# Ten units of a grouped convolution moved between the steps of the last attention stage

## The chip, the cores and the metric

The kernel runs on one core of a Trainium2 chip. The metric is the time on the device in microseconds. The profile is of one execution; its span is 3171.0 us, and that execution was measured at 3172.86 us.

## The reference

Two layers work on two images of 256 channels and 64 x 64 pixels, all in 32-bit floating point.

Layer 0 is a masked global attention with 8 heads of 32 channels over 4096 pixels:

```
q, k, v = Wq x, Wk x, Wv x                       (1x1 convolutions)
fuse    = softmax(q k^T / sqrt(32)) v            (per image and head)
x       = (Wf [x, fuse]) * m + x * (1 - m)       (m: mask resized to 64 x 64)
```

Layer 1 multiplies x by a channel gate (two small matrices and a sigmoid), runs an attention inside windows of 8 x 8 pixels (4 heads of 64 channels), adds it to x, shuffles the channels, and ends with two grouped 7 x 7 convolutions whose groups have 4 channels:

```
y   = relu(bn1(conv7x7(x, sa_w1)))               (256 -> 64 channels, 64 groups)
y   = bn2(conv7x7(y, sa_w2))                     (64 -> 256 channels, 64 groups)
out = x * sigmoid(y)
```

## The kernel before, in words

A first part, up to about 160 us, projects q, k and v and writes them to DRAM. It also prepares the convolution weights. The rest is one function, `pipeline`, of which the program holds two versions (arm a without, arm b with a subtracted row maximum). The data of this case take arm a, and its tiles carry an a at the end of their names.

**Attention.** `pipeline` walks over 512 slots: 2 images x 8 chunks of 512 pixels x 2 groups of four heads x 32 blocks of 128 keys. A slot multiplies keys with queries (`scores`, tile sa), takes the exponential on ACT (ea), multiplies with the values (`products`, ava) and adds the exponentials on DVE (suma). The order of the instructions is the order in which the Python code emits them; nothing reorders them later, and each engine goes through its own list in order.

**Stages.** When a chunk of an image is through all its keys, small actions with a delay in slots follow (`at`, `later`): the denominators (dna), their reciprocal, their spread over the channels (rda), and the multiplication. Then a generator, `stage`, carries the chunk through the rest of layer 0 and through layer 1 up to the convolutions: fusion (hya), channel gate (ca1a, ca2a), window attention (qka, vwa, sca, ewa, pta, oa), output projection (opa), and the sum xo, which is written to a DRAM tensor `x_s` (xs). It has twelve steps, one each time it yields. During attention one step is emitted every four slots, so the stage of a chunk is hidden under the attention of the next. The last chunk of the second image has no next one: its denominators and its stage run alone.

**Convolutions.** `convolve` then runs 16 units. A unit has 4 output groups of the shuffled channels for both images. Rows lie on partitions: 128 partitions hold four sub-channels of 30 image rows and a margin, and three overlapping row blocks cover an image, so both images are 2 x 3 x 64 = 384 columns. A unit does:

- `load_x`: its rows from `x_s` into one of four x buffers (xca), one load of 420 KB for each image, on SP's queue
- `load_w`: banded weights of 896 KB (wa), eight units ahead, on SP's queue
- `conv1`: 28 matmuls into one PSUM bank (c1a), then a relu on ACT into one of two y buffers (yca)
- `conv2`: 28 matmuls into four banks (c2a), then two tanh and one scaling on ACT into one of two z buffers (za)
- `gate`: one multiplication of z by x on DVE, then 24 output DMAs, 12 issued from SP and 12 from POOL

The first convolution of unit u + 1 is emitted ahead of the second of unit u. The x buffer of unit u is free after its gate, and the loads of unit u + 4 are issued on SP after the twelve outputs of unit u. The profile counts each of these 32-bit matmuls as two, so a convolution shows as 56 of them.

The buffers of the convolutions lie where the attention had its keys, values, queries and exponentials. They can be filled only when the attention is over. POOL zeroes the four x and two y buffers then.

Of the kernel before, what the change touches and what calls it, by code (L numbers as in the profile page):

```python
# [28 lines left out]
NPIECE = NMB // PB  # L29
AHEAD = 2  # L30
EB = 5
WB = 8
HEADS1, HD1 = 4, 64
WS = 8
NW = W // WS
# [19 lines left out]
def conv_seq_kernel(ctx: ExitStack, tc: tile.TileContext, a, out):  # L55
# [411 lines left out]


    def pipeline(arm, shifted, pools):
        fp, xpool, gp, wp, avp = pools  # L470

        att = ExitStack()
        kvp = att.enter_context(tc.tile_pool(name=f"kv{arm}", bufs=AHEAD + 1))
# [120 lines left out]
        def products(i):  # L594
# [16 lines left out]
            if stop:  # L611
                if g == 0:
                    fts[b, c] = fp.tile([P, KC, CH], F32, tag="f", name=f"f{arm}_{b}_{c}")
                f = fts[b, c]
                nc.scalar.copy(f[:, g, :], av)  # L615
                if g == 0:
                    return
                both = [totals.pop((b, c, gg)) for gg in range(KC)]
                inv = fp.tile([P, P], F32, tag="inv", name=f"inv{arm}_{i}")
                rd = fp.tile([P, KC, 4, P], F32, tag="rd", name=f"rd{arm}_{i}")  # L620


                def denominators():
                    s = psum2(f"dn{arm}_{i}")
                    for h in range(HEADS0):
                        for q in range(4):
                            r = slice(32 * q, 32 * q + 32)
                            nc.tensor.matmul(
                                s[r, 0, 0:P],
                                keysum[:, h].rearrange("p i h -> p (i h)"),  # L630
                                both[h // HG][:, h % HG, q * P : (q + 1) * P],
                                start=(h == 0),
                                stop=(h == HEADS0 - 1),
                            )
                    nc.scalar.copy(inv, s[:, 0, 0:P])


                def spread(hh):
                    t = psum2(f"rd{arm}_{i}_{hh}")
                    for gg in range(KC):  # L640
                        for q in range(2):
                            r = slice(64 * hh + 32 * q, 64 * hh + 32 * q + 32)
                            nc.tensor.matmul(
                                t[:, q, gg * P : gg * P + P],
                                spread_h[r, gg].rearrange("p j d -> p (j d)"),
                                inv[r, :],
                                start=True,
                                stop=True,
                            )
                    nc.scalar.copy(  # L650
                        rd[:, :, 2 * hh : 2 * hh + 2, :],
                        t[:, :, 0 : KC * P].rearrange("p q (g n) -> p g q n", g=KC),
                    )

                at(2, denominators)
                at(3, lambda: nc.vector.reciprocal(inv, inv))
                at(4, lambda: spread(0))
                at(5, lambda: spread(1))
                at(6, lambda: nc.vector.tensor_mul(f, f, rd.rearrange("p g q n -> p g (q n)")))
# [207 lines left out]

        def convolve():  # L870
            psum_layout(f"conv{arm}", 3, 1)
            pool = att.enter_context(tc.tile_pool(name=f"conv{arm}", bufs=1))
            nb = len(BLOCKS)


            xcs, ycs = [], []
            for u in range(4):
                t = pool.tile([P, B * nb, UG, WP], F32, name=f"xc{arm}{u}")
                nc.gpsimd.memset(t, 0.0)
                xcs.append(t)  # L880
            for u in range(2):
                t = pool.tile([P, B * nb, WP], F32, name=f"yc{arm}{u}")
                nc.gpsimd.memset(t, 0.0)
                ycs.append(t)
            xs, ws, ys = {}, {}, {}
            dst = out.rearrange("b (g i) r w -> b i r g w", i=4)
            n64 = B * nb * W

            def load_w(u):
                if u < NU:  # L890
                    t = pool.tile([P, 2 * 32 * UW], F32, tag="w", name=f"w{arm}{u}", bufs=WB)
                    nc.sync.dma_start(t, w_s[u])
                    ws[u] = t

            def load_x(u, b):
                if u < NU:
                    x = xs[u] = xcs[u % len(xcs)]
                    nc.sync.dma_start(
                        x[:, nb * b : nb * b + nb].rearrange("p n g w -> p n (g w)"),
                        x_s[b, :, :, UG * u : UG * u + UG, :].rearrange("n p g w -> p n (g w)"),  # L900
                    )

            def conv1(u):
                if u >= NU:
                    return
                x = xs[u]
                w = ws[u][:, 0 : 32 * UW].rearrange("p (m g d) -> p g d m", g=UG, d=KS)
                s = psum1(f"c1{arm}{u}")
                for d in range(KS):
                    for j in range(4):  # L910
                        nc.tensor.matmul(  # L911
                            s[32 * j : 32 * j + 32, 0:n64],
                            w[:, j, d, :],
                            x[:, :, j, d : d + W],
                            start=(d == 0),
                            stop=(d == KS - 1),
                        )
                y = ys[u] = ycs[u % 2]
                nc.scalar.activation(
                    y[:, :, PAD : PAD + W],  # L920
                    s[:, 0:n64].rearrange("p (n x) -> p n x", x=W),
                    AF.Relu,
                    bias=cbias1[:, u : u + 1],
                )

            def conv2(u):
                y = ys.pop(u)
                w = ws.pop(u)[:, 32 * UW :].rearrange("p (m d) -> p d m", d=KS)
                tiles = [psum2(f"c2{arm}{u}_{hh}") for hh in range(2)]
                for d in range(KS):  # L930
                    for j in range(4):
                        r = slice(32 * j, 32 * j + 32)
                        nc.tensor.matmul(  # L933
                            tiles[j // 2][:, j % 2, 0:n64],
                            w[r, d],
                            y[r, :, d : d + W],
                            start=(d == 0),
                            stop=(d == KS - 1),
                        )
                z = pool.tile([P, 4, n64], F32, tag="z", name=f"z{arm}{u}", bufs=2)  # L940
                for hh in range(2):
                    nc.scalar.activation(  # L942
                        z[:, 2 * hh : 2 * hh + 2, :], tiles[hh][:, :, 0:n64], AF.Tanh, scale=0.5
                    )
                nc.scalar.activation(z, z, AF.Copy, bias=0.25, scale=0.25)  # L945
                return z.rearrange("p j (n x) -> p j n x", x=W)

            def gate(u, z):
                x = xs.pop(u)
                nc.vector.tensor_mul(  # L950
                    z, z, x[:, :, :, PAD : PAD + W].rearrange("p n g x -> p g n x")
                )
                for b in range(B):
                    for n, (x0, r0, r1) in enumerate(BLOCKS):
                        for i in range(4):
                            p = 32 * i + 1 - x0
                            eng = nc.sync if i >= 2 else nc.gpsimd
                            eng.dma_start(  # L958
                                dst[b, i, r0:r1, UG * u : UG * u + UG, :],
                                z[p + r0 : p + r1, :, nb * b + n, :],  # L960
                            )


            for b in range(B - 1):
                for u in range(len(xcs)):
                    load_x(u, b)
            for u in range(WB):
                load_w(u)
            yield
            for u in range(len(xcs)):  # L970
                load_x(u, B - 1)
            conv1(0)
            for u in range(NU):
                conv1(u + 1)
                z = conv2(u)
                load_w(u + WB)
                gate(u, z)
                for b in range(B):
                    load_x(u + len(xcs), b)

        def run_later():
            for _ in range(len(later)):
# [18 lines left out]
            scores(i)()  # L1001
        for i, (b, c, g, m) in enumerate(slots):
            now[0] = i
            if m % PB == 0:
                load_piece(i // PB + AHEAD)
            if g == KC - 1 and m == 0:
# [11 lines left out]
                next(banded, None)  # L1018
            if i % 4 == 0:
                run_stages()  # L1020
        while later:
            now[0] += 1
            run_later()
        psum.close()
        att.close()
        conv = convolve()
        next(conv)
        while stages:
            run_stages()
        for _ in conv:  # L1030
            pass
        psum.close()
# [2 lines left out]
    def arm(name, shifted):  # L1035
        with (
# [2 lines left out]
            tc.tile_pool(name=f"g{name}", bufs=1) as gp,  # L1039
            tc.tile_pool(name=f"w{name}", bufs=1) as wp,  # L1040
            tc.tile_pool(name=f"av{name}", bufs=1, space=PSUM) as avp,
            tc.manual_schedule(),
        ):
            pipeline(name, shifted, (fp, xpool, gp, wp, avp))

    safe = nc.values_load(flag[0:1, 0:1], min_val=0, max_val=1)
    with tc.If(safe > 0) as cond:
# [68 lines left out]
```

## Time and profile before

Three runs took 3169.08, 3174.86 and 3179.28 us; the median is 3174.86.

| engine | busy us | share of the span |
|---|---|---|
| PE (matmul) | 3054.3 | 96% |
| PEld (weight load, overlaps PE) | 1031.8 | 33% |
| DVE | 2552.5 | 80% |
| ACT | 2369.6 | 75% |
| POOL | 350.1 | 11% |

| stretch, us from the start | what runs | PE busy us | granted PE clock |
|---|---|---|---|
| 2724 to 2908 | attention of the last chunk, stage of the one before | 181.7 of 184 | 1.00 |
| 2908 to 2976 | denominators and stage of the last chunk | 42.0 of 68 | 0.75 |
| 2976 to 2989 | writing xo, loading the first rows of the second image | 0.6 of 13 | 0.65 |
| 2989 to 3151 | convolutions of 16 units | 156.9 of 162 | 0.97 to 1.00 |
| 3151 to 3171 | last gate and the last outputs | 0.1 of 20 | 0.57 |

Times in the profile are microseconds from the start of the span unless marked ns. A line of the timeline gives start, duration, engine, line of the kernel, operation, output and inputs, number of instructions merged, and in brackets the idle time before it with what ended it. A line of stretches gives, for each stretch, its length and the busy time and instruction count of PE, PEld, DVE, ACT and POOL, then the granted PE clock, the mean busy share of the 16 DMA engines and the GB/s that they moved. A line of a group gives the count, the total busy time and the mean of one in ns, and the idle time before. SPq stands for the queue on which SP issues DMAs; its duration is that of issuing, not of the transfer. PE being busy doesn't mean that it runs at its peak, since matmuls are pipelined and a slow clock makes them longer.

### The profile page before, as it was taken

How to read it: one execution, taken by the hardware profiler on the slowest of the kernel's cores; microseconds unless marked ns; L12 is line 12 of the kernel's file. 1: busy time of each engine (PE TensorE's matmuls, PEld its weight loads, DVE VectorE, ACT ScalarE, POOL GpSimd, SP SyncE). 2: the span in 40 equal slices, each digit the busy share in tenths (PEclk: the TensorE clock that was granted, in tenths of full speed). 3: DMA queues.
4: the chain of work that ended last, by engine and by line, in shares of the span. 5: the costliest groups of instructions: out<-in, count | busy, mean ns of one | idle time of the engine just before them, and what ended most of it. 6: DMA issues, size and time to landing. Idle time of an engine off the chain costs nothing.

```text
span 3171.0 us, 58707 instructions
## 1 busy us (share of the span) xinstructions
PE 3054.3 (96%) x24330; PEld 1031.8 (33%) x24330; DVE 2552.5 (80%) x1372; ACT 2369.6 (75%) x3574; POOL 350.1 (11%) x595
## 2 busy tenths in 40 slices
PE   8989999999999999999999999999999999998697
PEld 4442332323223232322322323223232323222365
DVE  3239989899898989898989899898989898987111
ACT  2239878787878888888888787878888888886233
POOL 7112001011020000000000000000000000001066
PEclk9989999999999999999999999999999999999798
DMA  6856124334261313122222221211312132222374
GB/s 201 338 158 80 55 64 62 67 65 65 63 77 57 74 58 74 57 68 64 58 67 58 64 65 54 69 56 61 75 57 74 57 74 57 62 64 76 108 213 109
DMA packets 160341, 264.04 MB, mean 83 GB/s; under 512 B 43945, under 2 KB 62621, under 8 KB 160065
## 3 DMA queue, kind: packets, MB, share of 16 engines
q1 hardware_dynamic: 133664, 221.72, 23.5%
q0 software_dynamic: 22432, 35.91, 7.8%
q8 instruction: 193, 3.16, 0.4%
q10 hardware_dynamic: 3968, 2.57, 0.3%
q14 instruction: 84, 0.68, 0.1%
HBM read 197.89 MB, written 65.21 MB: 83 GB/s over the span
## 4 chain that ended last, share of the span: by engine, by line
PE 56%; DVE 26%; issue 7%; DMA 4%; ACT 4%; POOL 2%; SPq 1%; DVEq 0%; ACTq 0%; POOLq 0%
DVE suma L607 23%; PE sa L576 21%; PE ava L605 18%; PE qka L741 3%; PE hya L672 3%; ACT ea L586 3%; PE vwa L759 2%; PE opa L837 1%; PE q L219 1%; DMA out_dram<-za 1%; PE k L219 1%; POOL out_dram L958 1%; PE v L244 1%; DMA ks<-kst 1%; PE c2a L933 1%
## 5 line engine op out<-in xcount | busy, mean ns | idle before, releaser
L607 DVE TENSOR_TENSOR suma<-suma,ea 128x2048 f32<-128x2048 f32 x960 | 2199.0, 2291 | 99.4 <-ACT ea L586 12.3
L586 ACT ACTIVATE ea<-sa 128x512 f32<-128x512 f32 (+1 forms) x3072 | 2044.6, 748 | 182.8 <-DVE suma L607 116.6
L576 PE MATMUL sa<-qa,ka 32*128 32x512 f32 x8192 | 1250.1, 641 | 13.0 <-DMA va<-vs 7.8
L605 PE MATMUL ava<-ea,va 128*32 128x512 f32 x8192 | 1093.0, 605 | 4.4 <-ACT fa L615 4.4
L576 PEld LDWEIGHTS sa<-qa,ka 32*128 32x128 f32 x8192 | 370.1, 183 | 803.0 <-ACT ea L586 676.8
L605 PEld LDWEIGHTS ava<-ea,va 128*32 128x32 f32 x8192 | 161.6, 108 | 784.8 <-issue 753.8
L863 POOL DMA_DIRECT2D xs<-xo x94 | 65.8, 707 | 2486.1 <-DVE xo L848 2486.1
L950 DVE TENSOR_TENSOR za<-za,xca 128x1536 f32<-128x1536 f32 x16 | 28.1, 1759 | 149.3 <-ACT za L945 70.7
L741 PE MATMUL qka<-ua,qkv_w 128*128 128x512 f32 x256 | 121.1, 617 | 2.6 <-DVE ua L733 2.6
L958 POOL DMA_DIRECT2D out_dram<-za x192 | 107.9, 571 | 77.0 <-DVE za L950 62.4
L750 ACT ACTIVATE qka<-qka,qkv_b 128x512 f32<-128x512 f32 x64 | 40.5, 683 | 89.2 <-PE qka L741 89.2
L911 PE MATMUL c1a<-xca,wa 128*32 128x384 f32 x896 | 79.5, 504 | 17.5 <-DMA xca<-xs 14.8
L680 ACT ACTIVATE ta<-hya,bf 128x512 f32<-128x512 f32 x32 | 20.2, 683 | 101.1 <-PE hya L672 101.1
L788 DVE TENSOR_REDUCE mxwa<-ewa 128x16 f32<-128x1024 f32 x16 | 19.5, 1220 | 93.0 <-ACT ewa L786 93.0
L607 DVE TENSOR_TENSOR suma<-ea,ea 128x2048 f32<-128x2048 f32 x32 | 73.1, 2285 | 14.9 <-DMA mca<-masks 14.9
L684 DVE TENSOR_TENSOR ta<-ta,mca 128x512 f32<-128x512 f32 x32 | 22.0, 688 | 74.6 <-ACT ta L680 74.6
L231 ACT ACTIVATE qsq<-q,bq 128x512 f32<-128x512 f32 x32 | 22.0, 687 | 79.0 <-DVE qst L230 77.5
L933 PE MATMUL c2a<-yca,wa 32*128 32x384 f32 x896 | 79.9, 498 | 0.3 <-ACT za L942 0.3
L428 POOL DMA_DIRECT2D ws<-r2s x112 | 69.3, 622 | 61.7 <-DMA ws<-r2s 29.6
L933 PEld LDWEIGHTS c2a<-yca,wa 32*128 32x128 f32 x896 | 71.1, 303 | 10.7 <-issue 9.0
L942 ACT ACTIVATE za<-c2a 128x768 f32<-128x768 f32 x32 | 24.2, 809 | 66.2 <-DMA out_dram<-za 34.2
L741 PEld LDWEIGHTS qka<-ua,qkv_w 128*128 128x128 f32 x256 | 47.2, 194 | 76.7 <-issue 49.1
(137 smaller groups left out, 1615.0 us busy)
## 6 DMA issues: line engine op xcount, KB each, us to landing
ka<-ks SPq DMA_DIRECT2D x256, 256.0 KB
va<-vs SPq DMA_DIRECT2D x256, 256.0 KB
ws<-zero POOLq DMA_DIRECT2D x16, 896.0 KB, 22.8
wa<-ws SPq DMA_DIRECT2D x16, 896.0 KB
xca<-xs SPq DMA_DIRECT2D x32, 420.0 KB
xs<-xo POOLq DMA_DIRECT2D x78, 140.0 KB, 6.4
x<-in_x_dram SPq DMA_DIRECT2D x16, 512.0 KB
ks<-kst SPq DMA_DIRECT2D x32, 256.0 KB
```

Source lines behind the costliest of these rows:

```text
L219: nc.tensor.matmul(s[:, g, :], w[:, kc, g * P : (g + 1) * P], rhs, start=(kc == 0), stop=(kc == KC - 1),)
L428: nc.gpsimd.dma_start(band2[:, at0 : at0 + step * (n - 1) + 1 : step, :], spread(r2_s[k : k + 1, :, i], n),)
L576: nc.tensor.matmul(heads[j], k[r, cols], q[r, g, :], start=True, stop=not shifted)
L586: nc.scalar.activation(e[:, h, :], tile, AF.Exp, scale=SCALE0)
L605: nc.tensor.matmul(av[r, :], v[:, m % PB, r], e[:, j, :], start=start, stop=stop)
L607: nc.vector.tensor_add(total, first[0] if m == 1 else total, e)
L672: nc.tensor.matmul(s[:, oc, :], wf[:, kc, oc * P : (oc + 1) * P], xw[kc] if kc < KC else f[:, kc - KC, :], start=(kc == 0), stop=(kc == 2 ...
L741: nc.tensor.matmul(s[:, j, :], wqkv[:, kc, o : o + P], u[:, kc, :], start=(kc == 0), stop=(kc == KC - 1),)
L863: eng.dma_start(x_s[b, n, p + r0 : p + r1].rearrange("r g w -> g r w"), xo[64 * h : 64 * h + 64, oc, r0 - WS * c : r1 - WS * c, :],)
L911: nc.tensor.matmul(s[32 * j : 32 * j + 32, 0:n64], w[:, j, d, :], x[:, :, j, d : d + W], start=(d == 0), stop=(d == KS - 1),)
L933: nc.tensor.matmul(tiles[j // 2][:, j % 2, 0:n64], w[r, d], y[r, :, d : d + W], start=(d == 0), stop=(d == KS - 1),)
L958: eng.dma_start(dst[b, i, r0:r1, UG * u : UG * u + UG, :], z[p + r0 : p + r1, :, nb * b + n, :],)
```

## The change

The convolutions become 26 items in place of 16 units. Items 0 to 9 are units 0 to 9 of the first image alone, items 10 to 19 the same units of the second image alone, and items 20 to 25 are units 10 to 15 of both images as before. An item of one image has 192 columns, 12 output DMAs (6 from SP, 6 from POOL) and one x load.

- The generator `convolve` is started in the last chunk's attention: it zeroes the two y buffers and loads the rows of units 0 to 2 of the first image and the weights of unit 0. Its buffers for these come from a pool of their own that exists all the time. There are three x buffers in place of four, and they are not zeroed.
- The first convolution of item 0 is emitted right after the last matmuls of the attention, ahead of the denominators. After the denominators the attention's buffers are given up, the weights of units 1 to 9 are loaded into nine buffers (eight before), and the first convolution of item 1 is emitted.
- Then one piece of the convolutions (a `conv1`, or a `conv2`; the gate with its outputs and the next x load goes ahead of the `conv1`) is emitted after each remaining action and each step of the stage: `conv2` of item 0 ahead of the spread of the denominators, and so on, up to `conv1` of item 9 after the output projection.
- After the stage's last step, `conv2` of item 8 and its gate follow, then the first x loads of the second image, `conv1` of item 10, `conv2` of item 9 and the rest of the items.
- The weights of units 1 to 9 stay until the second image has used them. The weights of units 10 to 15 are each loaded after the gate of unit 1 to 6 of the second image, ahead of the next x load.

```diff
-WB = 8
+WB = 9
+EARLY = 10
...
+        items = [(u, (b,)) for b in range(B) for u in range(EARLY)]
+        items += [(u, tuple(range(B))) for u in range(EARLY, NU)]
+        staged = []
...
-            for u in range(4):
-                t = pool.tile([P, B * nb, UG, WP], F32, name=f"xc{arm}{u}")
-                nc.gpsimd.memset(t, 0.0)
-                xcs.append(t)
+            for k in range(3):
+                xcs.append(cpool.tile([P, B * nb, UG, WP], F32, name=f"xc{arm}{k}"))
...
+            def load_rows(k):
+
+                while len(xs) < min(k + 1, len(items)) and (
+                    staged or B - 1 not in items[len(xs)][1]
+                ):
+                    load_x(len(xs))
...
-            for u in range(NU):
-                conv1(u + 1)
-                z = conv2(u)
-                load_w(u + WB)
-                gate(u, z)
-                for b in range(B):
-                    load_x(u + len(xcs), b)
+            load_rows(len(xcs) - 1)
+            load_w(0)
+            yield
+            conv1(0)
+            pool = yield
+            for u in range(1, 1 + WB):
+                load_w(u)
+            for k, (u, images) in enumerate(items):
+                while len(xs) <= k + 1 < len(items):
+                    yield
+                    load_rows(k + 1)
+                conv1(k + 1)
+                yield
+                z = conv2(k)
+                yield
+                gate(k, z)
+                if B - 1 in images and u:
+                    load_w(u + WB)
+                load_rows(k + len(xcs))
...
+            if (b, c, g, m) == (B - 1, NCHUNK - 1, 0, 0):
+                conv = convolve()
+                next(conv)
...
-        while later:
+        now[0] += 1
+        run_later()
+        next(conv)
+        while totals:
             now[0] += 1
             run_later()
         psum.close()
         att.close()
-        conv = convolve()
-        next(conv)
-        while stages:
+        psum_layout(f"conv{arm}", 3, 1)
+        conv.send(att.enter_context(tc.tile_pool(name=f"late{arm}", bufs=1)))
+        while later or stages:
+            now[0] += 1
+            run_later()
             run_stages()
+            if later or stages:
+                next(conv)
+        staged.append(True)
         for _ in conv:
             pass
```

## The prediction

> **What bounds the kernel now.** I read the page first. Its second part has PE in the nines in nearly every slice, then a dip near the end. Next come busy times by stretch around that dip:
>
> ```profile
> core 0: us, PE busy (x) PEld busy (x) DVE busy (x) ACT busy (x) POOL busy (x), PEclk, DMA share, GB/s
> 2724.00:2908.00 184.00, 181.74 (x1483) 54.23 (x1478) 167.42 (x85) 153.12 (x234) 8.29 (x12) 1.00 0.23 59
> 2908.00:2976.00 68.00, 41.96 (x347) 23.18 (x338) 20.37 (x16) 12.92 (x20) 6.60 (x6) 0.75 0.34 134
> 2976.00:2989.00 13.00, 0.59 (x4) 0.24 (x8) 1.29 (x2) 1.15 (x2) 1.39 (x2) 0.65 0.46 115
> 2989.00:3054.00 65.00, 64.25 (x728) 42.51 (x720) 8.80 (x5) 19.11 (x22) 31.24 (x56) 0.97 0.54 163
> 3054.00:3102.00 48.00, 43.91 (x512) 30.05 (x509) 8.79 (x5) 17.43 (x20) 31.23 (x57) 1.00 0.70 207
> 3151.00:3171.00 20.00, 0.12 (x2) 0.00 (x0) 1.76 (x1) 2.55 (x3) 12.88 (x24) 0.57 0.28 57
> ```
>
> Attention fills PE until 2908. Then comes an 80 us hole (the last stage, a serial chain at a half-warm clock), then 162 us of convolutions, then 20 us in which only outputs leave. The change works on all three. The reader should see that the hole is not empty: PE is busy 42 of 68 us, partly because the clock is 0.75.
>
> What paces the convolutions is in the timeline of one turn of an x buffer, in the middle stretch:
>
> ```profile
> 3047.76 1.76 DVE L950 TENSOR_TENSOR za<-za,xca 128x1536 f32<-128x1536 f32 x1 [7.81 <-DMA out_dram<-za]
> 3050.50 9.33 SPq L958 DMA_DIRECT2D out_dram<-za  x12
> 3059.88 0.92 SPq L898 DMA_DIRECT2D xca<-xs  x2
> 3064.72 4.81 PE L911 MATMUL c1a<-xca,wa 128*32 128x384 f32 x56 [0.80 <-DMA xca<-xs]
> ```
>
> The gate of unit 4 frees x buffer 0, SP issues twelve outputs, only then the two loads of unit 8, and PE waits for them: 15.2 us from gate end to conv1. This loop goes round four buffers, so it barely binds. Units start 9.65 us apart when PE sets the pace and 10.5 to 11.5 us apart where the loop does. Last, the parts of a unit, from the groups by form and the lines of the weight tile:
>
> ```profile
> L911 PEld LDWEIGHTS c1a<-xca,wa x896: 132/137/177, 2988.4 to 3139.6; 128*32 128x32 f32 x180
> L933 PEld LDWEIGHTS c2a<-yca,wa x896: 298/302/325, 3001.1 to 3150.3; 32*128 32x128 f32 x180
> L933 PE MATMUL c2a<-yca,wa 32*128 32x384 f32 x896 | 79.9, 498 | 0.3 <-ACT za L942 0.3
> L933 PEld LDWEIGHTS c2a<-yca,wa 32*128 32x128 f32 x896 | 71.1, 303 | 10.7 <-issue 9.0 <-ACT za L942 0.8
> ```
>
> For c2, weight loads run 71.1 of the 79.9 us of its matmuls: they are just hidden under 384 columns.
>
> **What the Trainium skill says.** *TensorE: Matmul & The Clock Gate*, "LDWEIGHTS", makes a load's time a matter of its columns. The trace agrees (about 190 ns for 128 columns, 110 for 32, both contiguous) and adds that c2's weights, read 28 bytes apart, take 302. The same page, "What's actually happening", halves the clock after an idle window. Here the first conv1, after 12.6 us of idling, takes 7.22 us instead of 4.83. *DMA: Bandwidth & Descriptors*, "Issuing engines are not separate DMA queues", has all issuers share the 16 engines; the DMA share of 0.70 in the middle stretch fits. *Perfetto Trace Analysis*, "Identifying Performance Opportunities", reads a bubble that repeats on an engine as too few buffers; the trace shows such bubbles already with four x buffers (0.80, 1.43 and 1.87 us at 3064, 3085 and 3097). After the change there are three.
>
> **The change part by part** (all against the profiled span of 3171.0; the runs read 3169 to 3179, median 3174.9).
>
> *Sizes.* Ten units are split by image: 192 columns instead of 384. A conv1 of 384 is 14 rounds of 0.328 us plus 0.23. With half the stream, 14 x 0.164 + 0.25 = 2.55 us; its loads (0.16 us per round) just fit. For c2 the stream would give 2.6 us, the loads at their full 302 ns 4.5. Loads overlap somewhat (contiguous 128-column loads of 190 ns follow each other every 0.12 to 0.13 us), so I scale 302 ns to 0.25 us per round: 3.85 us, ends 2.6 and 4.5. So a split unit costs 6.4 us per image, 12.8 for both, where it cost 9.65: about 31 us more PE work over ten units. After c2 there are tanh 1.0, copy 0.8, gate 0.9 and hand-overs (half of 1.51, 1.49 and 1.76, a little over), together 2.75 us. Six outputs on SP take 2.75 us (twelve took 5.04 to 5.82 where nothing held them), POOL's six 3.4.
>
> *Before the hole.* Three x loads, w0 and the two y memsets move into attention: 2.2 MB is 5.2 us at the 420 GB/s reached at 2930, ahead of k and v loads issued two pieces (some 19 us) early. I take nothing; bound 5. The four x memsets (5.8 us on POOL) go; denominators and stage chain hide them.
>
> *The hole.* PE's order is fixed: conv1 of unit 0 right after attention, while DVE still sums (free); denominators end at 2919.5; then conv1 of unit 1, in front of everything in the chain. Its weights wait for the attention buffers, released at 2919.5 as the memset of x was before. Issue, about 1.8 us until bytes moved then, 2.2 us for 917 KB: conv1(1) at about 2924.0, cold. From there PE runs one conv piece between every two stage steps: eight conv1 (5.0 cold + 7 x 2.55 = 22.9), eight conv2 (8 x 3.85 = 30.8), the stage's matmuls warm (0.5, 0.5, 6.9, 1.05, 1.05, 3.63, 3.63, 3.65, 1.15, 2.1, 1.15, 3.7 = 29.0). Waits add 3.6: 2.7 for x of unit 3, whose issue sits on SP behind nine weight loads, 20 us of transfers; 0.9 for unit 8. Sum 86.2, so the output projection ends at 3010.2, where it ended at 2975.8: **34 us later**. Some of the stage's ACT and DVE work queues behind tanh and gates (exp waits for tanh of unit 5), but PE is the longer queue. Ends: 20 later with c2 at stream speed, 40 with full loads.
>
> *End of the stage.* Before, 12.6 us passed from there to the first conv1 of the second image. After, that load is issued behind the six outputs of unit 8, which wait for conv1(9) 2.55, conv2(8) 3.85, ACT and DVE 2.75, SP 2.75; then load and landing 4.0: 15.9 us. It starts at **3026.1** against 2988.4.
>
> *Second image and both.* With three buffers, x of item k+3 is issued after the gate of item k, which follows conv1(k+1) and conv2(k). So two starts later, conv1(k+3) waits for 2.55 + 3.85 + 2.75 + 2.75 + 0.46 + 3.8 = 16.2 us. Where a weight load is issued in front of it (units 1 to 6, 917 KB), 0.42 for issue and 1.5 of its 2.2 us make 18.1. That is 8 to 9 us per split unit, where PE needs 6.4. Starts after 3026.1: 8.9, 18.6, 25.1, 36.7, 43.2, 54.8, 61.3, 72.9, 79.4, then the both-image units at 90.2, 98.9, 109.7. For those the loop is 4.8 + 4.9 + 4.75 + 5.6 + 0.92 + 3.8, 24.8 us per two: 123.7, 134.5, 148.5; the last conv2 ends at 163.5. Before it was 162.2. Image 0's work is out of this phase, and nothing is gained, because the loop has fewer buffers and shorter turns to hide the same latency.
>
> *Tail.* From the last conv2, 4.75 + 0.3 + 6.7 (POOL) + 7.1 to the end as before = 18.9; before 20.4, as POOL was one unit behind.
>
> Sum: 3026.1 + 163.5 + 18.9 = 3208.5, or **37.5 us more**. A measured time lies 1.9 above its span in the profiled run: 3210.
>
> **The rivals.**
> - *PE sets the pace of the second image* (faster). Loads land within PE's own time: the projection ends at its early bound, 20 us later (2995.8), the second image starts 13.7 after it, at 3009.5; cold start 2.4, conv2(9) 2.6, ten units of 5.0, six of 9.75, total 113.5; tail 18.9: 3142, time 3144. It decides if everything after conv2 (gate, outputs, landing, 9.8 us) takes no more than one PE unit, 5.0 to 6.4. For it: the added work lies in a hole that was 40% idle. Against it: no landing in the trace is under 3.4 us from issue (2984.93 to 2988.41 on an empty queue).
> - *Halves are cheap, the loop is at its floor* (about the same). c2 2.7, ACT and DVE 2.6, SP 2.6, landing 3.6: 7.0 us per unit, 8.0 with weights. The stage is 22 us late, the phase takes 145 instead of 162, the tail saves 1.5: span 3174, time 3176.
> - *The loop is slower still.* PE idles 3 to 5 us per pair; if the clock drops (the transposes took 3.68 after 7.6 us of idling, 2.08 warm) and full weight loads hold (4.5), a split unit takes 10 us: 3235.
> - That the change doesn't do what it says is excluded: the order of the instructions shows the conv pieces between the steps.
>
> **How the numbers follow.** Forecast case (3190 to 3222) 0.61, cheap halves 0.15, slower loop 0.13, PE pace 0.11. Faster by over 0.3% (under 3165; about what this kernel's measurement can tell from no change): the PE pace and a sliver of cheap halves, 0.13. Within 0.3%: most of cheap halves, 0.13. Slower: 0.74. The range 3168 to 3236 leaves out the faster cases and the far end of the slow one.
>
> **What would show it.** The output projection ending near 3010; conv1 of 192 columns at 2.5 and conv2 at 3.9 us; c1 waiting on xca in most of the second image's units, at a spacing near 8 to 9 us; PE busy about 75% there. A spacing of 5 to 6.5 us, or a stage delayed by 20 us or less, makes it wrong on the fast side.

## The result and the profile after

The changed kernel takes 3228.61 us (median of four runs, 3227.55 to 3229.07). The four runs of the kernel before that it is set against have a median of 3177.07 us (3169.08 to 3183.15). The ratio is 1.0163, with a 95% interval from 1.0139 to 1.0187: the change makes the kernel **1.6% slower**. The forecast was 3210, with a range of 3168 to 3236.

Below, each kernel is compared through its own ratio to the runs of before that were made beside it, because the median of before differed by up to 8 us between sets of runs (3177, 3173, 3169). Places in time are from one profiled execution of each; the span of the changed kernel is 3225.8 us.

The stretches of the changed kernel, with the same columns as those of before (length, busy time of PE, PEld, DVE, ACT and POOL, granted PE clock, DMA share, GB/s):

```profile
core 0: us, PE busy (x) PEld busy (x) DVE busy (x) ACT busy (x) POOL busy (x), PEclk, DMA share, GB/s
2724.00:2908.00 184.00, 181.74 (x1484) 53.73 (x1480) 167.53 (x84) 154.59 (x236) 8.19 (x13) 1.00 0.27 70
2908.00:2976.00 68.00, 51.43 (x666) 36.34 (x663) 24.10 (x18) 17.92 (x33) 11.15 (x20) 0.85 0.46 160
2976.00:3010.00 34.00, 32.77 (x603) 27.11 (x605) 8.28 (x9) 13.25 (x21) 13.50 (x24) 1.00 0.30 70
3040.00:3100.00 60.00, 45.58 (x747) 38.78 (x744) 6.72 (x7) 14.98 (x28) 20.22 (x36) 0.86 0.45 132
```

The attention's last chunk (first row) is what it was: PE is busy for 181.74 of 184 us in both kernels. The stage that follows is fuller, but also longer. And where before had a convolution phase at a clock of 0.97 to 1.00 with PE busy 64 of 65 us, PE now idles for a quarter of the time (45.6 of 60 us) and is granted 0.86.

Three of the costliest PE groups of the page, kept apart by shape (count, busy us, mean ns, then the idle time ahead of them by what ended it), say which operation pays:

```profile
L951 PE MATMUL c2a<-yca,wa 32*128 32x192 f32 x1120 | 72.3, 401 | 0.0
L927 PE MATMUL c1a<-xca,wa 128*32 128x192 f32 x1120 | 64.9, 390 | 41.6 <-DMA xca<-xs 30.7 <-issue 6.2 <-DMA wa<-ws 4.7
L927 PE MATMUL c1a<-xca,wa 128*32 128x384 f32 x336 | 33.2, 551 | 16.2 <-DMA xca<-xs 16.2
```

The first convolution waits for rows of x, 30.7 us ahead of the split units and 16.2 us ahead of those for both images. The second one waits for nothing. The same from PE's view, the waits between 2905 and 3226 us (total us, times, longest):

```profile
PE c1a L927 <- DMA xca<-xs: 47.0, 11, 9.3
PE c1a L927 <- issue: 6.2, 1, 6.2
PE c1a L927 <- DMA wa<-ws: 4.7, 1, 4.7
```

One such wait in the timeline, with what stands ahead of it on the other engines:

```profile
3073.54 3.57 PE L951 MATMUL c2a<-yca,wa 32*128 32x192 f32 x56
3077.03 2.53 PE L927 MATMUL c1a<-xca,wa 128*32 128x192 f32 x56
3079.50 3.58 PE L951 MATMUL c2a<-yca,wa 32*128 32x192 f32 x56
3088.61 4.71 PE L927 MATMUL c1a<-xca,wa 128*32 128x192 f32 x56 [5.53 <-DMA xca<-xs]
...
3078.92 0.96 DVE L973 TENSOR_TENSOR za<-za,xca 128x768 f32<-128x768 f32 x1 [13.16 <-ACT za L967]
3079.91 2.46 SPq L979 DMA_DIRECT2D out_dram<-za  x6
3082.47 0.36 SPq L899 DMA_DIRECT2D wa<-ws  x1
3082.87 0.43 SPq L906 DMA_DIRECT2D xca<-xs  x1
```

The gate frees the x buffer at 3079.88. SP issues six outputs, a weight load and then the x load, which is landed 5.3 us after its issue ended. PE could have used the rows at 3083.08, when conv2 was through; it stood still for 5.53 us. The conv1 that follows takes 4.71 us, where the one that finds PE running takes 2.53. The same columns of stretches, for the wait and for that conv1:

```profile
3083.10:3088.60 5.50, 0.00 (x0) 0.03 (x1) 0.96 (x1) 1.71 (x3) 2.91 (x6) 0.88 0.89 282
3088.61:3093.25 4.64, 4.64 (x57) 2.90 (x57) 0.00 (x0) 0.00 (x0) 0.90 (x2) 0.50 0.87 257
```

While PE waits the clock is still granted at 0.88; in the conv1 behind the wait it is 0.50. Below, *cold* means an operation that runs at such a lowered clock after idling, and *warm* one at the full clock of 1.00.

The whole difference of the two spans, 54.8 us, in sections:

| section | before | forecast | after | after less before |
|---|---|---|---|---|
| start to the end of the attention (copy of fa starts) | 2908.7 | 2908.7 | 2914.3 | +5.6 |
| to the end of the output projection | 67.1 | 101.5 | 103.1 | +36.0 |
| to the first conv1 of the second image | 12.6 | 15.9 | 15.3 | +2.7 |
| to the end of the last conv2 | 162.7 | 163.5 | 173.6 | +10.9 |
| to the end | 19.9 | 18.9 | 19.5 | -0.4 |

The first row can't be told from scatter, so it isn't shown to be an effect of the change. The copy of fa starts at 2903.8, 2906.4, 2908.2, 2909.2 and 2908.1 in the profiles of experiments 1, 2, 3, 4 and 6, all of which have the changed kernel's attention (experiment 2 with six smaller x loads in it); before's 2908.7 lies among them. Experiment 5, which has the attention of before, starts it at 2903.2, 5.5 us away from before itself.

### The profile page after: what moved, and what is told of

It is laid out like the page before. It is cut to its first block, busy times and chain, and to the rows that moved or that the text cites. A ratio compares the mean times of both kernels' runs of the same rounds, so it can differ in the third digit from the quotient of the medians.

```text
span 3225.8 us, 61120 instructions
## 1 busy us (share of the span) xinstructions
PE 3085.0 (96%) x25450; PEld 1077.1 (33%) x25450; DVE 2554.2 (79%) x1382; ACT 2376.3 (74%) x3614; POOL 344.5 (11%) x591
## 4 chain that ended last, share of the span: by engine, by line
PE 55%; DVE 27%; ACT 4%; issue 4%; DMA 2%; SPq 1%; POOL 0%; DVEq 0%; ACTq 0%
DVE suma L609 24%; PE sa L578 20%; PE ava L607 18%; PE qka L745 4%; PE hya L676 4%; ACT ea L588 3%; PE c1a L927 2%; PE c2a L951 2%; PE vwa L763 2%; PE opa L841 2%; DMA xca<-xs 1%; DMA ka<-ks 1%; SPq L979 1%; PE rda L647 1%; PE ca2a L719 0%
## 5 line engine op out<-in xcount | busy, mean ns | idle before, releaser
L609 DVE TENSOR_TENSOR suma<-suma,ea 128x2048 f32<-128x2048 f32 x960 | 2199.0, 2291 | 103.7 <-ACT ea L588 16.7
L973 DVE TENSOR_TENSOR za<-za,xca 128x768 f32<-128x768 f32 (+1 forms) x26 | 29.7, 1144 | 215.3 <-ACT za L967 184.9
L927 PE MATMUL c1a<-xca,wa 128*32 128x192 f32 (+1 forms) x1456 | 98.1, 427 | 57.8 <-DMA xca<-xs 47.0
L745 PE MATMUL qka<-ua,qkv_w 128*128 128x512 f32 x256 | 118.4, 605 | 0.0
L951 PE MATMUL c2a<-yca,wa 32*128 32x192 f32 (+1 forms) x1456 | 102.6, 424 | 0.3 <-ACT za L961 0.3
L951 PEld LDWEIGHTS c2a<-yca,wa 32*128 32x128 f32 x1456 | 94.5, 317 | 11.4 <-issue 10.2
L927 PEld LDWEIGHTS c1a<-xca,wa 128*32 128x32 f32 x1456 | 65.0, 148 | 86.7 <-issue 72.4
L935 ACT ACTIVATE yca<-c1a,cbias 128x192 f32<-128x192 f32 (+1 forms) x26 | 11.9, 459 | 109.5 <-PE c1a L927 109.5
L684 ACT ACTIVATE ta<-hya,bf 128x512 f32<-128x512 f32 x32 | 20.2, 683 | 97.8 <-PE hya L676 97.8
L961 ACT ACTIVATE za<-c2a 128x384 f32<-128x384 f32 (+1 forms) x52 | 26.6, 562 | 80.1 <-PE c2a L951 49.0
L792 DVE TENSOR_REDUCE mxwa<-ewa 128x16 f32<-128x1024 f32 x16 | 19.5, 1220 | 82.8 <-ACT ewa L790 82.8
```

The source lines that it names most:

```text
L609: nc.vector.tensor_add(total, first[0] if m == 1 else total, e)
L745: nc.tensor.matmul(s[:, j, :], wqkv[:, kc, o : o + P], u[:, kc, :], start=(kc == 0), stop=(kc == KC - 1),)
L927: nc.tensor.matmul(s[32 * j : 32 * j + 32, 0 : n * W], w[:, j, d, :], xs[k][:, 0:n, j, d : d + W], start=(d == 0), stop=(d == KS - 1),)
L951: nc.tensor.matmul(tiles[j // 2][:, j % 2, 0 : n * W], w[r, d], y[r, 0:n, d : d + W], start=(d == 0), stop=(d == KS - 1),)
```

## The experiments

**The theory.** Two costs of about one size. First, the convolution pieces are put between the steps of a serial chain and lengthen it by nearly all their PE time, and what they save later is their own PE time, so the move by itself gains little. Second, three x buffers can't hide the turn from gate to landed rows, so the second phase, with ten units' worth of one image gone, is not shorter. **The rivals:** that splitting units makes PE work dear (strided weight loads under half a stream), and that the pieces between the steps are themselves what is lost.

### 1. A fourth x buffer

```diff
             pool = yield
+            xcs.append(pool.tile([P, B * nb, UG, WP], F32, name=f"xc{arm}3"))
             for u in range(1, 1 + WB):
```

> The changed kernel with a fourth x buffer, which comes from the pool that opens after the attention. Theory (the turn of an x buffer paces the convolutions): the turn of about 20 us, measured over two starts in the changed kernel, is spread over three, 6.7 us, or PE's own 6.1 if the clock stays up. The ten items of the second image take 61 to 68 us in place of 96, the six of both about 62 in place of 77; the output projection ends at most 5 us earlier (x of item 3 no longer waits). Time 3175 to 3190. Rival (SP's issuing, the DMA engines or PE itself set the pace): the spacing of the second image's items stays above 9 us and the time within 6 us of 3229.

Measured: 3175.09 us, ratio 1.0015 (1.0005 to 1.0025). As the theory had it, except that x of unit 3 is still late: its conv1 in the hole waits 5.30 us (6.16 in the changed kernel), as its load still stands behind the nine weight loads on SP. PE's wait for x between 2905 and 3170 us:

```profile
PE c1a L927 <- DMA xca<-xs: 12.8, 4, 9.1
```

The two groups of conv1, by shape:

```profile
L927 PE MATMUL c1a<-xca,wa 128*32 128x192 f32 x1120 | 58.1, 359 | 21.8 <-DMA xca<-xs 11.2 <-issue 5.3 <-DMA wa<-ws 4.7
L927 PE MATMUL c1a<-xca,wa 128*32 128x384 f32 x336 | 28.9, 492 | 1.6 <-DMA xca<-xs 1.6
```

And the stretch from 3034 to 3150 us, in the columns of the stretches above:

```profile
3034.00:3150.00 116.00, 111.40 (x1654) 90.01 (x1652) 18.40 (x15) 39.14 (x60) 63.07 (x114) 1.00 0.58 163
```

The wait for x falls from 47.0 to 12.8 us, and the groups lose most of theirs. In the last line's stretch PE was busy for 89.5 us in the changed kernel at a clock of 0.86; with one buffer more it is 111.4, at a full clock. The ten items of the second image take 66.8 us (96.1 in the changed kernel), and the phase up to the last conv2 129.2 (173.6). So this one buffer is worth nearly the whole loss. But the projection still ends 102.4 us after the attention. Against before, the hole costs 35.3 us more and the phase behind it 33.5 less: the move, freed of its missing buffer, gains nothing.

### 2. The same three buffers, cut in halves

An item of one image fills only half of a buffer that was laid out for two. Here an item of one image gets half a buffer, so six loads fit where three did; items of both images get whole ones.

```diff
-                x = xs[k] = xcs[k % len(xcs)]
+                h = part(k)
+                if len(h) == 2:
+                    x = xs[k] = xcs[h[0] // 2]
+                else:
+                    x = xs[k] = xcs[h[0] // 2][:, nb * (h[0] % 2) : nb * (h[0] % 2) + nb]
...
-                load_rows(k + len(xcs))
+                load_rows(ahead(k))
```

> The changed kernel with each of the three x buffers cut in two for items of one image, so that six such items find room; items of both images still have three. No memory is added. Theory: single items go at PE's pace, 6.1 us, so the second image's ten take about 62 us in place of 96; items of both images keep their 26 us per two. x of item 3 is there early, so the output projection ends about 6 us earlier. Time 3180 to 3195. Rival (landings are slow because the DMA engines are shared, whatever the number of buffers): still over 8 us per item, time above 3215.

Measured: 3176.38 us, ratio 1.0015 (1.0006 to 1.0025), a little better than expected. The groups of conv1 by shape:

```profile
L941 PE MATMUL c1a<-xca,wa 128*32 128x192 f32 x1120 | 55.4, 347 | 14.1 <-DMA xca<-xs 9.3 <-DMA wa<-ws 4.8
L941 PE MATMUL c1a<-xca,wa 128*32 128x384 f32 x336 | 33.6, 555 | 10.7 <-DMA xca<-xs 10.7
```

From its second start on, the second image's items start 5.96 to 5.99 us apart, which is PE's pace for conv1 and conv2, and none of those waits. The both-image items still have three buffers, still wait (10.7 us) and still take 25 to 27 us per two. No memory was added. So it is the number of loads that may be under way that decides, not the size of the memory behind them. The load of unit 3, late in the changed kernel, is here ahead of the nine weight loads; no conv1 waits for rows in the hole, and the projection ends 94.4 us after the attention.

### 3. Contiguous weights

Both convolutions read their weights from one tile, with the seven taps as the innermost index. Here the taps are outer and the 32 or 128 columns lie side by side. The weights are taken in another order than they were written, so the values differ; the number and the sizes of the instructions stay.

```diff
-                w = ws[u][:, 0 : 32 * UW].rearrange("p (m g d) -> p g d m", g=UG, d=KS)
+                w = ws[u][:, 0 : 32 * UW].rearrange("p (g d m) -> p g d m", g=UG, d=KS)
...
-                w = ws[u][:, 32 * UW :].rearrange("p (m d) -> p d m", d=KS)
+                w = ws[u][:, 32 * UW :].rearrange("p (d m) -> p d m", d=KS)
```

> The changed kernel, except that both convolutions read their weights as if the 128 or 32 columns of one tap lay side by side (they lie 28 or 112 bytes apart), so the taps are mixed up and the values of the output are others; the number and size of all instructions stay. Theory (the second convolution of 192 columns is bound by its strided weight loads): it falls from 3.57 us to about 2.6, its loads from 320 ns to below 200; the output projection ends 8 to 9 us earlier, each turn of an x buffer is 1 us shorter, together 12 to 18 us less: 3211 to 3217. Rival (3.57 us are streaming and overhead of the row tiles): no change of it, time within 4 us of 3229.

Measured: 3210.78 us, ratio 1.0123 (1.0106 to 1.0139). The groups of the split convolutions by shape:

```profile
L951 PE MATMUL c2a<-yca,wa 32*128 32x192 f32 x1120 | 53.6, 333 | 0.2 <-issue 0.2
L951 PEld LDWEIGHTS c2a<-yca,wa 32*128 32x128 f32 x1456 | 64.4, 187 | 21.3 <-issue 11.3 <-ACT za L961 0.9
L927 PE MATMUL c1a<-xca,wa 128*32 128x192 f32 x1120 | 65.0, 391 | 47.4 <-DMA xca<-xs 42.9 <-DMA wa<-ws 4.5
L927 PE MATMUL c1a<-xca,wa 128*32 128x384 f32 x336 | 37.0, 602 | 17.0 <-DMA xca<-xs 17.0
```

A split conv2 falls from 72.3 / 20 = 3.62 us to 53.6 / 20 = 2.68, so the stride of the weights was a real cost of splitting. PE is relieved of 18.7 us, but the ratio falls by only 0.004, some 13 us; and in the profiles 6.1 of the 13.2 us between the spans are the earlier end of the attention. So the time is just below the 3211 to 3217 expected, with scatter helping. The hole, for which 8 to 9 us less was expected, gets 3.1 us shorter. The 42.9 us of waiting hold 9.4 us in the hole, of which the 7.4 for unit 3 stand under "issue" in the changed kernel, so they can't be set against its 30.7. Counted from the second image's first conv1 on, the waits for x grow from 45.7 to 50.6 us, and the conv1 of both images take 37.0 us for 33.2. Of the 10 us that conv2 gives there, some 8.7 go that way, and the phase is only 2.7 us shorter (170.9 for 173.6). So the theory that splitting makes PE work dear is not wrong about the price, but with three buffers it isn't what bounds. Contiguous weights with enough buffers were not run.

### 4. The pieces behind the stage, not between its steps

```diff
-            if later or stages:
-                next(conv)
```

> The changed kernel without a piece of the convolutions between the last actions and steps of the stage: after the first convolution of items 0 and 1, which stay where they are, all pieces follow the stage. Theory (interleaving hides PE work in the hole but lengthens the chain by nearly as much PE time): the output projection ends about 76 us after the attention in place of 103, and the nine items of the first image then take 8 to 10 us each ahead of the second image's: time 3265 to 3285, so the interleaving by itself gains 40 to 55 us, and the loss against the kernel before comes from the splitting and the buffers. Rival (the interleaving itself is what costs): the time is at or below 3229.

Measured: 3246.71 us, ratio 1.0240 (1.0223 to 1.0257). The direction is right and the size is not. From PE's timeline, the projection and the start of the second image (second and third line: the last conv1 of the first image, the first of the second):

```profile
2975.95 3.70 PE L841 MATMUL opa<-ota,out_w 128*128 128x512 f32 x8 [0.81 <-ACT ota L830]
...
3040.94 4.20 PE L927 MATMUL c1a<-xca,wa 128*32 128x192 f32 x56 [3.12 <-DMA xca<-xs]
3048.58 2.54 PE L927 MATMUL c1a<-xca,wa 128*32 128x192 f32 x56
```

The projection is back at 70.4 us after the attention (67.1 before, 103.1 in the change). The remaining items of the first image then run by themselves, one every 8.3 us (2983.09 to 3040.94 is seven starts), and the second image starts at 3048.58, 139.4 us after the attention; in the changed kernel it was 118.4. So placing the pieces between the steps gains 21 us in the profile and 0.8% in the ratio, not the 40 to 55 us expected. Of what the pieces save behind the stage, 32.7 us come back as delay of the chain (103.1 against 70.4). That is two thirds of the 48 us that these fifteen pieces take on PE; the theory had nearly all of it. The gain holds for three buffers: at the 5.97 us per item of experiment 2 the seven starts would take 41.8 us in place of 57.9, which by this estimate would leave about 5 of the 21 us.

### 5. Before, with three buffers

The buffer count by itself, with no convolution moved.

```diff
-            for u in range(4):
+            for u in range(3):
```

> The kernel before with three x buffers in place of four, nothing else. Theory (the turn of an x buffer): the turn of 24 to 28 us is spread over two starts in place of three, so a unit of both images takes 12.5 to 14 us in place of 10.1 on average; 16 units: 40 to 55 us more, 3213 to 3228. Rival (four buffers were enough and three are too, as only three waits on x stood in the profile): within 5 us of the kernel before.

Measured: 3219.03 us, ratio 1.0157 (1.0139 to 1.0175), as expected. PE's wait for x:

```profile
PE c1a L911 <- DMA xca<-xs: 51.0, 8, 12.7
```

and one of these waits in the timeline:

```profile
3029.09 4.82 PE L911 MATMUL c1a<-xca,wa 128*32 128x384 f32 x56
3033.83 4.96 PE L933 MATMUL c2a<-yca,wa 32*128 32x384 f32 x56
3044.63 7.28 PE L911 MATMUL c1a<-xca,wa 128*32 128x384 f32 x56 [5.84 <-DMA xca<-xs]
```

The old kernel with the new one's buffer count shows the same pattern, one long wait in every two starts and a cold conv1 behind it, and loses as much as the whole change did. Together with experiment 1 this shows the cause from both sides.

### 6. Four buffers, six units early

Fewer pieces in the hole, the rest as in experiment 1.

```diff
-EARLY = 10
+EARLY = 6
```

> The kernel with four x buffers, with six units ahead in place of ten, placed as before from the first step on. Four units less are split (2.3 us of PE work each), and the pieces between the steps run out halfway. Theory (in the hole, PE is what the chain waits for): the output projection ends 20 to 24 us earlier (eight pieces of 2.5 and 3.5 us fewer), the convolutions after it take 13 to 17 us more: 3165 to 3172. Rival (the chain itself, not PE, sets the hole's length): the projection ends less than 8 us earlier and the time rises by 5 to 10 us.

Measured: 3189.36 us, ratio 1.0065 (1.0048 to 1.0082). **A miss**: slower than experiment 1, and above the 3165 to 3172 expected. PE's timeline, from the scores of the window attention (sca) on:

```profile
2984.70 1.16 PE L782 MATMUL sca<-qka 64*64 64x64 f32 x64
2993.48 3.68 PE L808 MATMUL pta<-ident,ewa 64*64 64x64 f32 x64 [7.62 <-DVE ewa L800]
3000.23 5.40 PE L841 MATMUL opa<-ota,out_w 128*128 128x512 f32 x8 [0.81 <-ACT ota L830]
3017.93 3.95 PE L927 MATMUL c1a<-xca,wa 128*32 128x192 f32 x56 [12.30 <-DMA xca<-xs]
3034.36 4.25 PE L927 MATMUL c1a<-xca,wa 128*32 128x192 f32 x56 [8.98 <-DMA xca<-xs]
```

I had taken the hole to shrink by what is taken out of it. Six pieces with 18 us of PE time are gone ahead of the projection, but it ends only 5 us earlier (97.5 us after the attention, 102.4 in experiment 1), and the phase from the second image's first conv1 to the last conv2 takes 22.2 us more (151.4 against 129.2), where 13 to 17 were expected. That is nearer to the rival, which had the chain itself set the hole's length, though the time rises by more than its 5 to 10 us. With one piece per step the pieces of six units are used up at 2981 us, but for conv2 of item 5, which stands behind the second image's first conv1. From there on the softmax leaves PE idle for 7.62 us, and the transposes and the projection run cold (3.68 and 5.40 us, warm 2.08 and 3.70). Nothing stands in the gap either in which xo is written and read back (12.30 us), and the second image's second load stands behind a gate (8.98 us). So it matters not only how many pieces there are, but behind which step each stands.

### 7. Pieces only where the chain leaves PE idle

Six units early. Conv1 of units 0 and 1 and conv2 of unit 0 go ahead of the denominators, with the weights of both loaded in attention (so no wait for weights is left). Then one piece each after steps 4 and 6 (fusion and channel gate), two around the softmax, and four after the stage's last step, while xo is written and read. The x buffers are halved as in experiment 2, and there is a fourth for the both-image items. The second image's loads go out ahead of those last pieces' outputs.

```diff
-EARLY = 10
+EARLY = 6
+STAGED = 2
...
-        now[0] += 1
-        run_later()
-        next(conv)
+        next(conv)
+        next(conv)
...
+        plan = {4: 1, 6: 1, 10: 1, 11: 1}
+        step = 0
...
-                next(conv)
+                for _ in range(plan.get(step, 0)):
+                    next(conv)
+            step += 1
...
+                if k == STAGED:
+                    load_rows(ahead(k - 1))
```

> Six units ahead, x buffers in halves for single items and a fourth one for items of both images, and the pieces put where the chain waits for ACT, DVE or a transfer: two first convolutions and one second one ahead of the denominators, while DVE still adds (so weights of unit 1 and the small z come early too); then one piece after the fusion, one after the channel gate, two around the softmax, and four (12 us) after the stage's last step, while xo is written and read back, with the x load issued ahead of their outputs. Theory: the pieces cost the chain at most 3 us and a warm clock gives back some 5, so the output projection ends about 62 to 70 us after the attention in place of 103 (67 in the kernel before), the second image starts without a stop, and the rest is 6 x 6.0 + 3.5 + 10 x 9.65: about 137 us in place of 162. Time 3138 to 3152. Rival (chain and pieces delay each other wherever the pieces lie): the projection ends over 80 us after the attention and the time is over 3160.

Measured: 3142.81 us (3139.45 to 3149.35), ratio **0.9927** (0.9906 to 0.9948). It beats both kernels. The stretch from 2908 to 2976 us:

```profile
2908.00:2976.00 68.00, 59.79 (x882) 44.28 (x884) 20.37 (x20) 22.49 (x37) 15.09 (x26) 1.00 0.46 158
```

and, from PE's timeline, one of the stage's operations (qka) in the kernel before and here:

```profile
2943.10 10.07 PE L741 MATMUL qka<-ua,qkv_w 128*128 128x512 f32 x16 [2.62 <-DVE ua L733]
...
2933.62 7.13 PE L746 MATMUL qka<-ua,qkv_w 128*128 128x512 f32 x16
```

The transposes, the projection, the second image's first conv1 and the last one that stops, all in this run:

```profile
2952.99 2.08 PE L809 MATMUL pta<-ident,ewa 64*64 64x64 f32 x64 [1.71 <-DVE ewa L801]
2958.14 3.70 PE L842 MATMUL opa<-ota,out_w 128*128 128x512 f32 x8 [0.81 <-ACT ota L831]
2974.76 2.55 PE L942 MATMUL c1a<-xca,wa 128*32 128x192 f32 x56 [0.96 <-DMA xca<-xs]
3033.10 6.50 PE L942 MATMUL c1a<-xca,wa 128*32 128x384 f32 x56 [3.34 <-DMA xca<-xs]
```

In the stretch that before spent with PE busy for 42.0 us at a clock of 0.75, PE is busy for 59.8 at 1.00. The pieces keep PE warm through the chain, and the projection ends 58.2 us after the attention, *sooner* than with no pieces at all (67.1). The second image's first conv1 waits 0.96 us. The phase up to the last conv2 takes 143.0 us (162.7). One stop over a microsecond is left there, at 3033.10. For the chain the timelines tell where the gain comes from: from the spread of the denominators to the projection, the stage's own matmuls take 29.4 us in place of 38.7, and the four pieces among them, 12.2 us of PE time, lie in what was idle time. For the whole, several things were changed at once, so the runs don't tell how the gain divides among placing, buffers, earlier loads and the smaller number of split units.

## Why the prediction was right, and where not

- **Direction and size.** The forecast of slower holds, and the time is 18.6 us above the number, inside the range. The forecast case (3190 to 3222) was just missed. Without the 5.6 us of the attention the time would lie midway between the forecast and the rival *The loop is slower still* (3235). Of the signs named ahead, the late projection, the conv1 of 2.5 us and PE busy for about 75% came; the second image's items are 9.6 us apart on average, over the 8 to 9 named. Of the 17.3 us by which the span exceeds the forecast's (3208.5), 5.6 are attention that the change doesn't touch, and 10.1 are the second phase.
- **Before the hole.** Nothing was taken for the loads that move into the attention, and PE waits for none of them there.
- **The hole.** Forecast 34.4 us more, measured 36.0. Its terms: conv1(1) waits for its weights and starts 4.7 us after the denominators end (forecast 4.5). Conv1 takes 2.53 to 2.55 us (2.55). Conv2 takes 3.58 (3.85), so the scaled load time was too high by 0.27 us, a little over 2 us in eight of them. The scaling was a guess: in proportion to the spacing it quotes (0.12 to 0.13 us for loads of 190 ns), 302 ns come to 0.20 us and conv2 to about 3.0; that 3.85 came nearer is luck. The loads that it reads as agreeing with the page (110 ns for 32 columns, 190 for 128) grow with the columns, but far less than in proportion. The wait for x of unit 3 was too low: 2.7 forecast, 6.16 measured, with a cold conv1 of 4.20 behind it. The load was held up behind the nine weight loads for longer than I took; experiment 2 shows that, as the wait is gone where the load goes ahead of them. These errors cancel in part, so that the hole's total is closer than its terms is luck too.
- **End of the stage and of the kernel.** 15.9 forecast, 15.3 measured, and 18.9 against 19.5 at the end. The forecast's 162.2 and 20.4 for before take the start of the last matmul for its end; they are 162.7 and 19.9.
- **The second phase: the term that was mis-sized.** The mechanism was as stated: x loads behind the gate, with one long wait per two starts. The forecast took 18.1 us for two starts with a weight load between; 19.7 is measured from 3068.89 to 3088.61. Added up from the timeline: conv1 4.65, conv2 3.49, ACT and DVE 2.85, outputs 2.6, weight and x issue 0.8, landing 5.3. The forecast's terms for these were 2.55, 3.85, 2.75, 2.75, 0.9 and 5.3. Only conv1 is clearly off upwards, by 2.1 us. **I had costed every conv1 of the loop warm**, although the wait that the same sum contains makes PE idle for 5 to 6 us in every such turn, and the cold conv1 (clock 0.50) stands inside the loop, so it feeds the next wait. That PE would drop its clock here stood only in the rival *The loop is slower still*. The ten items of the second image take 96.1 us for 90.2. The both-image items show the same: conv1 of 6.1 to 6.5 us for 4.8, 25 to 26 us per two for 24.8.
- **The rivals.** *PE sets the pace* needed all that follows conv2 (ACT and gate, outputs, landing) within one PE unit. It was 11.6 us (3077.03 to 3088.61, with a weight load; 9.8 was forecast without) against 6.0, so it didn't come; experiment 2 shows that pace with six loads under way. *Cheap halves* fell with the 5.3 us landing, though its price for conv2 of 2.7 us comes true with contiguous weights (2.68), and even then the time stays at 1.0123. *The slower loop* was right on the clock and wrong on the full weight loads (conv2 3.58, not 4.5). Its 10 us for a split unit is what pairs take from the third item on (19.6 to 20.2 us per two starts); pairs among the first four items take 16.6 to 16.7. Of the bubbles that the forecast reads as waits for x, the profile puts the third (1.87 us at 3097) down to an output.
- **What the prediction did not see.** It put the hole's growth down to PE being the longer queue for all of it. That holds in the changed kernel, but experiment 6 shows that where the pieces run out, from the softmax on, the chain itself sets the pace, and experiment 7 that pieces at the right steps shorten the chain. Nothing in the forecast told these two apart.

## What to carry to other kernels

Before work is cut into smaller items, work out one turn of each ring of buffers (free, issue queue, landing, use) against number of buffers times the time of an item: halving the items halves the time that each buffer may take, and latency doesn't shrink with them; loading halves of a buffer restores the balance at no memory. Cost the operation behind a repeated wait cold where the trace shows that waits of that length slow it, since that lengthens the next turn. Work that is to fill a serial chain goes only behind the steps after which the engine would idle, late ones among them; with a piece behind every step, two thirds of its time came back here as delay of the chain.

## What the runs showed of the hardware

- **Short idling is enough to make PE slow.** A split conv1 took 2.55 us after 0.96 us of idling (experiment 7), 4.20 after 2.99 (3049.32 in the changed kernel, clock 0.59) and after 3.12 (experiment 4), and in the changed kernel 4.71 to 4.72 after 5.53 to 5.90 (clock 0.50 in the two at 3068.89 and 3088.61). The length of the wait alone doesn't set it: in experiment 4 one conv1 took 3.93 us after 2.12 of idling (clock 0.62) and another 2.54 after 2.85 (clock 1.00), and in the changed kernel one took 4.15 after 9.28. The Trainium skill, *TensorE: Matmul & The Clock Gate*, "What's actually happening", has the clock halved after an idle window of about 3.4 us, and the windows run on freely instead of starting with the kernel. Waits of 2.1 to 3.1 us are shorter than such a window, and the conv1 behind several of them was already 1.4 to 1.7 us longer; here the measurement decides.
- **The stride of the weights costs load time.** 128 columns read 28 bytes apart took 317 ns per load on average, side by side 187 ns. With 384 columns to stream the load is all but hidden; with 192 it sets the time (3.62 us against 2.68).
- **Landing time of one 420 KB load.** 5.3 us after its issue where a weight load of 896 KB went ahead of it. The DMA engines' mean busy share of 0.45 in that stretch (3040 to 3100 us) hides how they work: while PE waited it was 0.89 (3083.1 to 3088.6), and in the 9 us before, from 3073.5 to 3082.5, it was 0.12.
- **The same code scatters.** In the profiles of the kernels that share the changed kernel's attention, its end lies between 2903.8 and 2914.3 us. In the latest of them PE stood 4.58 us for one load of keys in the middle of the attention (until 936 us), at a place that no edit touches. So in a single profile, a difference of 10 us far ahead of an edit tells nothing of it.
